# Features of the next batch in two-bank and single-bank PSUM tiles, and a product with Wa moved ahead of the ends

## The chip, the cores and the metric

The kernel runs on one core of a Trainium2 chip. The metric is the device time of one execution in microseconds; three runs of the kernel before gave 2164.74, 2165.57 and 2166.67, a median of 2165.57. The core has five queues that run in order: TensorE (PE) for matrix products and transposes, VectorE (DVE), ScalarE (ACT), GpSimd (POOL), which here only issues indirect DMAs, and SyncE (SP), which issues most plain DMAs.

## The reference

Two graph layers run over 16 batches of 1024 nodes with 256 features; `adj` is one sparse 1024x1024 matrix for all batches.

```python
feats = einsum('bni,oi->bno', data, W1)
f1 = einsum('bno,o->bn', feats, W2) + b2[0]
coefs = softmax(leaky_relu(f1[:, :, None] + f1[:, None, :]) + adj, axis=-1)
h = einsum('bij,bjo->bio', coefs, feats) + bias2 + data
# second layer, on h
pre_u = h @ W1[:d];  pre_v = h @ W1[d:]
S = sigmoid(relu(pre_u[:, :, None, :] + pre_v[:, None, :, :] + b1) @ W2 + b2)
a = einsum('buv,bud->bvd', S * adj, h)
m = einsum('uv,bud->bvd', adj, h) * h
z = beta1 * h + beta2 * (a @ Wa + ba) + beta3 * (m @ Wm + bm)
```

## The kernel before

**Order of the work.** The tile scheduler is switched off. A `Timetable` (line 347) keeps entries of a planned time and a function; `matmuls` (line 360) puts an entry at `now` and moves `now` on by the planned length of the columns. `run` sorts all entries by time and emits them. So the planned times fix only the order of the instructions on each queue; on the chip each queue runs in that order, as soon as its semaphores allow.

**Stages.** For every batch TensorE computes the features (`features`, line 986), eight chunks of 128 nodes in four pairs `c2`; each chunk is two matmuls (512 records in the trace for 256 matmuls) of 257 columns, 256 features and a last column that carries the node's logit. `keep_features` (line 999) clamps the last columns of a pair (`f`, VectorE, line 1004), takes an exponential of them (ScalarE, line 1008) and copies the two chunks to SBUF scaled by it (ScalarE, line 1016). `begin_f` (line 1389) turns the eight clamped columns into rows (`pr`, TensorE, line 965), takes their highest value (VectorE, line 973) and makes `row` and `col` (ScalarE, lines 979 to 984). `spread` (line 1023) makes eight weight tiles `eT` on VectorE; `attend` (line 1037, `pv`) multiplies them with the features; `keep_h` (line 1049) finishes a chunk of the layer's output h on VectorE.

Of h, `turn_h` (line 1057, `ph`) makes transposed pairs of chunks, copied by ScalarE (line 1072). For each pair i, `end` (line 1074, `pp`) computes the two products with the second layer's W1, side 0 copied by VectorE (line 1091) and side 1 by ScalarE (line 1093); `weighed` (line 1103, `pea`) computes the product with Wa, copied by ScalarE (line 1118). All three results go to DRAM through SP's queue. `message` (`pm`, line 1135) and `product` (`pz`, line 1154) make m and its product with Wm. Eight batches (`LATER`: 0 to 3 and 11 to 14) put the messages off to the end of the kernel, by storing h (`put_off`, line 1126); the others, 4 to 10, do them at once, spread over the next batch.

**Scores.** The edges of the graph are stored as 135 slots of 128 edges. For each of three groups of batches (0 to 4, 5 to 9, 10 to 15) and each slot, POOL gathers rows of the ends (`gv`, line 1200, and `gu`, line 1193), VectorE compares (line 1229), ScalarE reduces per batch (line 1243), and POOL scatters the results (line 1209). These steps are planned at an even pace over most of the kernel, so they stand between the other instructions of VectorE and ScalarE. The scores of a group start after its last batch; after the last batch, `gather` (line 1335, `pzg` and `pzh`) sums over scored edges.

**PSUM.** There are eight banks, in two pools: `p1` is a ring of four single banks (`pv`, `ph`, `pea`, `pm`, `pz`), `p2` a ring of two tiles of two banks each (transposed input `pt`, features `pf`, ends `pp`, rows `pr`, and `pzg` at the end). A new tile of a ring waits until the oldest one's readers are done.

**The place of the change** is the handover from batch b-1 to b. At the end of the pass for one batch, TensorE's order is: attention 6, `ph` (2), attention 7, the four pairs of features of the next batch, ends (2, 0), `ph` (3), `pr`. The next pass of the loop (line 1466) begins with `pea` (2), ends (2, 1), for batches 4 to 10 a message, ends (3, 0), ends (3, 1), `pea` (3), and then attention 0 of the new batch:

```python
weigh_ends(b - 1, 2)
one_end(b - 1, 2, 1)
if at_once:
    messages(b - 1, 0, 0)
one_end(b - 1, 3, 0)
one_end(b - 1, 3, 1)
weigh_ends(b - 1, 3)
```

In p2's ring the order here is: pairs 0 to 3, ends (2, 0), `pr`, ends (2, 1), (3, 0), (3, 1).

Of the kernel before, what the change touches and what calls it, by code (L numbers as in the profile page):

```python
# [8 lines left out]
F32 = mybir.dt.float32  # L9
AF = mybir.ActivationFunctionType  # L10
ALU = mybir.AluOpType
# [3 lines left out]
P = 128  # L15
BANK = 512
# [6 lines left out]
SPAN = 2500.0  # L23
# [348 lines left out]
def edge_layers(  # L372
# [36 lines left out]
    nc = tc.nc  # L409
    B, N, D = x.shape  # L410
# [10 lines left out]
    p1 = ctx.enter_context(tc.tile_pool(name="p1", bufs=4, space=PSUM))  # L421
    p2 = ctx.enter_context(tc.tile_pool(name="p2", bufs=2, space=PSUM))
# [484 lines left out]
    st = {}  # L907
# [76 lines left out]
        nc.scalar.activation(st["col"], st["f99"], AF.Exp, bias=st.pop("under"))  # L984

    def features(b, c2):
        pf = st["pf", c2] = p2.tile([P, 2, BANK], F32, tag="p2", name="pf")
        for i in range(2):
            c = 2 * c2 + i
            for h in range(H):  # L990
                nc.tensor.matmul(  # L991
                    pf[:, i, : D + 1],
                    lhsT=st["xT"][:, h, c * P : (c + 1) * P],
                    rhs=w1T[:, h, :],
                    start=(h == 0),
                    stop=(h == H - 1),
                )

    def keep_features(b, c2):
        if c2 == 0:  # L1000
            st["feats", b] = work.tile([P, C, D + 1], F32, name="feats")
            st["f99"] = two.tile([P, C], F32, name="f99")
        feats, f99, pf = st["feats", b], st["f99"], st.pop(("pf", c2))
        nc.vector.tensor_scalar(
            f99[:, 2 * c2 : 2 * c2 + 2], pf[:, :, D], -2.0 * SPAN, 2.0 * SPAN, ALU.max, ALU.min
        )

        nc.scalar.activation(
            feats[:, 2 * c2 : 2 * c2 + 2, D],
            f99[:, 2 * c2 : 2 * c2 + 2],  # L1010
            AF.Exp,
            scale=SLOPE / (1.0 - SLOPE),
        )
        for i in range(2):
            c = 2 * c2 + i
            nc.scalar.activation(  # L1016
                feats[:, c, :D], pf[:, i, :D], AF.Copy, scale=feats[:, c, D : D + 1]
            )
        if c2 == C // 2 - 1:
            nc.vector.tensor_tensor(f_most, f_most, f99, ALU.max)  # L1020
            nc.vector.tensor_tensor(f_least, f_least, f99, ALU.min)
# [52 lines left out]
    def end(b, i, side):  # L1074

        pp = st["pp", side] = p2.tile([P, 2, BANK], F32, tag="p2", name=f"pp{side}")
        for k in range(2):
            for h in range(H):
                nc.tensor.matmul(  # L1079
                    pp[:, k, :R],  # L1080
                    lhsT=st["hTi", b, i][:, h, k * P : (k + 1) * P],
                    rhs=wuv[:, side, h, :],
                    start=(h == 0),
                    stop=(h == H - 1),
                )

    def keep_end(b, i, side):
        e = two.tile([P, 2, R], F32, name=f"end{side}", tag="end", bufs=3)
        pp = st.pop(("pp", side))[:, :, :R]
        if side == 0:  # L1090
            nc.vector.tensor_tensor(e, pp, bu.unsqueeze(1).to_broadcast([P, 2, R]), ALU.add)
        else:
            nc.scalar.copy(e, pp)  # L1093
        g, j = member(b)
        rows = slice(2 * i * P, (2 * i + 2) * P)
        nc.sync.dma_start(
            out=(pu_d, pw_d)[side][g][rows, j * R : (j + 1) * R].rearrange(
                "(c p) k -> p c k", p=P
            ),
            in_=e,  # L1100
        )

    def weighed(b, i):
        pp = st["pea"] = p1.tile([P, 2, D], F32, tag="p1", name="pea")
        for k in range(2):
            for h in range(H):
                nc.tensor.matmul(  # L1107
                    pp[:, k, :],
                    lhsT=st["hTi", b, i][:, h, k * P : (k + 1) * P],
                    rhs=wa[:, h, :],  # L1110
                    start=(h == 0),
                    stop=(h == H - 1),
                )

    def keep_weighed(b, i):
        g, j = member(b)
        e = two.tile([P, 2, D], F32, name="ea")
        nc.scalar.copy(e, st.pop("pea"))
        nc.sync.dma_start(
            out=ha_d[g][2 * i * P : (2 * i + 2) * P, j * D : (j + 1) * D].rearrange(  # L1120
                "(c p) k -> p c k", p=P
            ),
            in_=e,
        )

    def put_off(b):

        nc.sync.dma_start(out=h_d[b], in_=held[b].rearrange("p c d -> p (c d)"))
# [6 lines left out]
    def message(b, half, h):  # L1135
        span = slice(half * BANK, (half + 1) * BANK)
        pm = st["pm", h] = p1.tile([P, BANK], F32, tag="p1", name="pm")
        for c in range(C):
            nc.tensor.matmul(  # L1139
                pm,  # L1140
                lhsT=held[b][:, c, h * P : (h + 1) * P],
                rhs=adj_sb[:, c, span],
                start=(c == 0),
                stop=(c == C - 1),
            )

    def keep_message(b, half, h):
        if h == 0:
            st["mT"] = dense.tile([P, H, BANK], F32, name="mT")
        nc.vector.tensor_tensor(  # L1150
            st["mT"][:, h, :], st.pop(("pm", h)), st["hT", b, half][:, h, :], ALU.mult
        )
# [252 lines left out]
    def grows(*chunks):  # L1405
        for c in chunks:
            end = times.matmuls(C * P, lambda c=c: turn_grown(c))
            times.at(end + 0.2, lambda c=c: keep_grown(c))

    def attention(b, c):  # L1410
        end = times.matmuls(C * (D + 1), lambda: attend(b, c))
        times.at(end + 0.6, lambda: keep_h(b, c))
# [5 lines left out]
    def one_end(b, i, side):  # L1418
        time = times.matmuls(4 * R, lambda: end(b, i, side))
        times.at(time + 0.3, lambda: keep_end(b, i, side))  # L1420

    def weigh_ends(b, i):
        time = times.matmuls(4 * D, lambda: weighed(b, i))
        times.at(time + 0.3, lambda: keep_weighed(b, i))
# [6 lines left out]
    def messages(b, half, h, delay=0.3):  # L1431
        time = times.matmuls(C * BANK, lambda: message(b, half, h))
        times.at(time + delay, lambda: keep_message(b, half, h))
# [32 lines left out]
    for b in range(B):  # L1466
        at_once = b > 0 and b - 1 not in LATER
        more = b + 1 < B

        if b:  # L1470
            weigh_ends(b - 1, 2)
            one_end(b - 1, 2, 1)
            if at_once:
                messages(b - 1, 0, 0)
            one_end(b - 1, 3, 0)
            one_end(b - 1, 3, 1)
            weigh_ends(b - 1, 3)
            if b - 1 in LATER:
                times.at(times.now, lambda b=b: put_off(b - 1))
            if any(b == lo for lo, _ in GROUPS):  # L1480
                started.append(times.now + 19.0)
        attention(b, 0)
        if b == 0:
            grows(6, 7)
        if at_once:
            messages(b - 1, 0, 1)
        attention(b, 1)
        spreads(b, 0)
        if more:
            times.at(times.now, lambda b=b: load_x(b + 1))  # L1490
        if at_once:
            products(b - 1, 0, 1)
        if b == 0:
            for i in range(2):
                for h in range(H):
                    times.matmuls(2 * R, lambda i=i, h=h: sort_columns(i, h))
            times.matmuls(2 * R, sort_bias)
        attention(b, 2)
        if at_once:
            messages(b - 1, 1, 0)  # L1500
        turned_ends(b, 0)
        attention(b, 3)
        spreads(b, 1)
        if at_once:
            messages(b - 1, 1, 1)
        both_ends(b, 0)
        attention(b, 4)
        if at_once:
            products(b - 1, 2, 3)
        if not more:  # L1510
            times.at(times.now, lambda: take_up(LATER[0]))
            times.at(times.now + 20.0, lambda: take_up(LATER[1]))
        turned_ends(b, 1)
        if more:
            begin(b + 1, 0)
        attention(b, 5)
        both_ends(b, 1)
        if more:
            begin(b + 1, 1)
        attention(b, 6)  # L1520
        turned_ends(b, 2)
        attention(b, 7)
        for c2 in range(C // 2):
            if more:
                begin_features(b + 1, c2)
        one_end(b, 2, 0)
        turned_ends(b, 3)
        if more:
            begin_f(b + 1)
# [58 lines left out]
    b = B - 1  # L1588
    for n in range(3):
# [5 lines left out]
        b = LATER[n]  # L1595
# [31 lines left out]
    for i, at in starts.items():  # L1627
        if i == 5:
            continue
        b = LATER[i]  # L1630
# [137 lines left out]
```

## Time and profile before

| | |
|---|---|
| median of three runs | 2165.57 us |
| the profiled execution | 2166.46 us, its span 2164.4 us |
| mean granted TensorE clock | 0.985 |
| DMA, whole span | 644.37 MB, 297 to 298 GB/s |
| DMA share 960 to 1080 us / 1500 to 1700 us | 0.82 / 1.00 |
| granted clock 1080 to 1150 us / 1290 to 1340 us | 0.93 / 1.00 |
| TensorE busy, 960 to 1080 us | 110.57 of 120 us |
| TensorE busy, 1290 to 1340 us | 50.00 of 50 us |

Times in the profile are counted from the start of the span. A line of a timeline has the start, the duration, the engine, the line of the kernel, the operation, what it writes and reads, and how many instructions were merged; a bracket gives the idle time before it and what ended it. A "remote" release is one whose queue the profile does not know. A line of waits names who waited for whom, with the total, the number and the longest. In a group's line, busy time and mean duration of one stand before the bar, and after it the engine's idle time just before those instructions, with its main releasers.

### The profile page before, as it was taken

The page shows a single profiled execution, that of the slowest core. Times are in us where ns is not written, and L with a number is a line of the kernel's source. Part 1 is how long each engine was busy: PE and PEld are TensorE (multiplying, and loading weights), DVE is VectorE, ACT ScalarE, POOL GpSimd, SP SyncE. Part 2 cuts the span into 40 slices and gives each one's busy share as a digit, 9 for nine tenths or more (in the row PEclk, how much of TensorE's full clock was granted, in tenths as well). Part 3 has the DMA queues.
Part 4 walks back from the last instruction along what each step waited for, and adds up shares of the span by engine and source line. Part 5 has one row for each costly group of instructions (what it writes and reads, how often), then busy time and mean ns, then how long its engine had stood idle before and what let it go on. Part 6 is the DMA issues. An engine that isn't in the chain of part 4 may idle for free.

```text
span 2164.4 us, 28928 instructions
## 1 busy us (share of the span) xinstructions
PE 2054.0 (95%) x8566; PEld 1561.6 (72%) x8566; DVE 1565.5 (72%) x2316; ACT 1378.6 (64%) x4842; POOL 1128.4 (52%) x986
## 2 busy tenths in 40 slices
PE   6999999999999999989899899999999999999998
PEld 5887888777676767667678777456666767667887
DVE  6798875577767676667667776577888978885544
ACT  4212222476767767576777787468888788885554
POOL 2121221267666676667666668665767666674000
PEclk8999999999999999999999999999999999999999
DMA  6587776788877787788888889899999999997774
GB/s 211 201 328 292 287 294 249 257 267 274 282 260 256 262 277 249 270 282 268 267 298 283 270 276 341 310 344 413 392 388 384 402 410 385 368 396 276 266 240 134
DMA packets 248007, 644.37 MB, mean 298 GB/s; under 512 B 37154, under 2 KB 137506, under 8 KB 245794
## 3 DMA queue, kind: packets, MB, share of 16 engines
q0 software_dynamic: 82528, 349.79, 46.4%
q1 hardware_dynamic: 129474, 258.44, 32.5%
q10 hardware_dynamic: 35840, 34.22, 4.6%
q8 instruction: 69, 1.13, 0.2%
q14 instruction: 96, 0.79, 0.1%
HBM read 479.56 MB, written 162.92 MB: 297 GB/s over the span
## 4 chain that ended last, share of the span: by engine, by line
PE 56%; DVE 15%; issue 9%; DMA 7%; ACT 7%; POOL 3%; another core or an unknown queue 2%; ACTq 0%; POOLq 0%; DVEq 0%
PE pv L1041 16%; PE pm L1139 10%; PE pp L1079 9%; PE pzg L1344 7%; DVE gv L1229 6%; DMA gv<-pw_d,idx_v 6%; ACT gv L1243 4%; PE pea L1107 4%; PE pf L991 3%; PE pzh L1344 3%; PE pz L1159 2%; DVE apart L1331 2%; POOL sa_d L1209 2%; POOL gv L1200 1%
## 5 line engine op out<-in xcount | busy, mean ns | idle before, releaser
L1243 ACT ACTIVATE gv<-gv 128x272 f32<-128x272 f32 x2058 | 856.4, 419 | 301.5 <-DVE gv L1229 152.6
L1229 DVE TENSOR_TENSOR gv<-gv,gu 128x680 f32<-128x680 f32 (+1 forms) x810 | 705.5, 907 | 106.3 <-DMA gv<-pw_d,idx_v 101.4
L1200 POOL DMA_INDIRECT gv<-pw_d,idx_v x405 | 481.1, 1188 | 386.3 <-ACT gv L1243 248.6
L1209 POOL DMA_INDIRECT sa_d<-lg,idx_s x405 | 496.1, 1225 | 131.5 <-issue 112.5
L1041 PE MATMUL pv<-feats,eT 128*128 128x257 f32 x2048 | 468.6, 381 | 5.1 <-DVE eT L1028 3.5
L1139 PE MATMUL pm<-adj_sb,xh 128*128 128x512 f32 x1024 | 450.0, 592 | 1.8 <-DVE xh L1055 1.8
L1041 PEld LDWEIGHTS pv<-feats,eT 128*128 128x128 f32 x2048 | 382.0, 190 | 67.6 <-DVE eT L1028 9.6
L1344 PE MATMUL pzg<-ha_g,apart 128*128 128x256 f32 x1536 | 370.5, 384 | 25.0 <-DVE apart L1331 18.3
L1243 ACT ACTIVATION_READ_ACCUMULATOR gv<-gv 128x1 f32 x2058 | 389.2, 189 | 0.0
L1344 PEld LDWEIGHTS pzg<-ha_g,apart 128*128 128x128 f32 x1536 | 287.7, 190 | 91.2 <-DVE apart L1331 35.6
L1139 PEld LDWEIGHTS pm<-adj_sb,xh 128*128 128x128 f32 x1024 | 193.1, 190 | 220.0 <-issue 217.2
L1326 ACT COPY apart<-sat 128x640 f32<-128x640 f32 (+1 forms) x192 | 264.4, 1391 | 87.8 <-PE pzh L1344 46.7
L1079 PE MATMUL pp<-wuv,hT 128*128 128x272 f32 x1024 | 257.9, 402 | 20.6 <-ACT end L1093 7.1
L1331 DVE TENSOR_TENSOR apart<-apart,adj_sb 128x640 f32<-128x640 f32 (+1 forms) x192 | 165.9, 866 | 118.0 <-ACT apart L1326 112.5
L1079 PEld LDWEIGHTS pp<-wuv,hT 128*128 128x128 f32 x1024 | 196.4, 194 | 75.6 <-ACT end L1093 10.4
L1028 DVE SCALAR_TENSOR_TENSOR eT<-row,col,grown 128x512 f32<-128x512 f32 x256 | 183.1, 745 | 28.0 <-ACT col L984 25.1
L843 POOL DMA_INDIRECT table_d<-rec,at x52 | 57.5, 1106 | 267.2 <-DVE rec L836 160.4
L991 PE MATMUL pf<-w1T,xT 128*128 128x257 f32 x512 | 128.6, 405 | 30.6 <-ACT feats L1016 25.5
L1072 ACT COPY hT<-ph 128x512 f32<-128x512 f32 x96 | 55.2, 576 | 147.8 <-PE ph L1061 90.3
L991 PEld LDWEIGHTS pf<-w1T,xT 128*128 128x128 f32 x512 | 101.5, 202 | 54.5 <-ACT feats L1016 32.9
L1159 PE MATMUL pz<-wm,mT 128*128 128x256 f32 x512 | 118.1, 384 | 6.0 <-DVE mT L1150 5.3
L1107 PE MATMUL pea<-wa,hT 128*128 128x256 f32 x512 | 122.3, 382 | 0.0
(184 smaller groups left out, 1616.2 us busy)
## 6 DMA issues: line engine op xcount, KB each, us to landing
sa_d<-zero SPq DMA_DIRECT2D x128, 512.0 KB
sat<-sa_d SPq DMA_DIRECT2D x128, 320.0 KB
sat<-sa_d SPq DMA_DIRECT2D x64, 384.0 KB
pu_d<-end SPq DMA_DIRECT2D x64, 272.0 KB
pw_d<-end SPq DMA_DIRECT2D x64, 272.0 KB
xh<-in_x_dram SPq DMA_DIRECT2D x16, 1024.0 KB
ha_d<-ea SPq DMA_DIRECT2D x64, 256.0 KB
zb_d<-zb ACTq DMA_DIRECT2D x64, 256.0 KB
```

The costliest lines, as they stand in the source:

```text
L991: nc.tensor.matmul(pf[:, i, : D + 1], lhsT=st["xT"][:, h, c * P : (c + 1) * P], rhs=w1T[:, h, :], start=(h == 0), stop=(h == H - 1),)
L1041: nc.tensor.matmul(pv[:, : D + 1], lhsT=st["eT", b, k, j // 4][:, j % 4, i * P : (i + 1) * P], rhs=st["feats", b][:, j, :], start=(j == 0) ...
L1079: nc.tensor.matmul(pp[:, k, :R], lhsT=st["hTi", b, i][:, h, k * P : (k + 1) * P], rhs=wuv[:, side, h, :], start=(h == 0), stop=(h == H - 1),)
L1107: nc.tensor.matmul(pp[:, k, :], lhsT=st["hTi", b, i][:, h, k * P : (k + 1) * P], rhs=wa[:, h, :], start=(h == 0), stop=(h == H - 1),)
L1139: nc.tensor.matmul(pm, lhsT=held[b][:, c, h * P : (h + 1) * P], rhs=adj_sb[:, c, span], start=(c == 0), stop=(c == C - 1),)
L1200: nc.gpsimd.indirect_dma_start(out=gv, out_offset=None, in_=pw_d[g], in_offset=bass.IndirectOffsetOnAxis(ap=idx_v[:, t, s : s + 1], axis=0),)
L1209: dma = nc.gpsimd.indirect_dma_start(out=sa_d[g], out_offset=bass.IndirectOffsetOnAxis(ap=idx_s[:, t, s : s + 1], axis=0), in_=lg[:, i, : ...
L1229: nc.vector.tensor_tensor(mv, mv, mu, op)
L1243: nc.scalar.activation(one[:, j, :], one[:, j, :], AF.Copy, accum_out=lg[:, i, j : j + 1])
L1326: nc.scalar.copy(apart.rearrange("p g v -> p v g"), sat)
L1331: nc.vector.tensor_tensor(apart, apart, a.unsqueeze(1).to_broadcast([P, SIZE[g], P]), ALU.mult)
L1344: nc.tensor.matmul(st["pzg", g, vc][j // 4][:, j % 4, :], lhsT=apart[:, j, :], rhs=ha, start=(c == 0 and j % 2 == 0), stop=(c == C - 1 and ...
```

## The change

In `features`, pairs 0 and 1 stay in two-bank tiles of p2. Each chunk of pairs 2 and 3 gets a single bank of p1, four in all. `keep_features` clamps the last column of both chunks of a pair in one VectorE instruction where they share a tile, and in two instructions of one column each where they don't. The rest of it is the same, with another operand. In the handover, `pea` (3) is emitted ahead of ends (3, 0) and (3, 1) where the batch's messages are put off, and stays behind them where they are made at once.

```diff
     def features(b, c2):
-        pf = st["pf", c2] = p2.tile([P, 2, BANK], F32, tag="p2", name="pf")
+        if c2 < 2:
+            both = p2.tile([P, 2, BANK], F32, tag="p2", name="pf")
+            pfs = [both[:, 0, : D + 1], both[:, 1, : D + 1]]
+            st["pf", c2] = [both[:, :, D]], pfs
+        else:
+            pfs = [p1.tile([P, BANK], F32, tag="p1", name="pf1")[:, : D + 1] for _ in range(2)]
+            st["pf", c2] = [pf[:, D:] for pf in pfs], pfs
...
-                    pf[:, i, : D + 1],
+                    pfs[i],
...
-        feats, f99, pf = st["feats", b], st["f99"], st.pop(("pf", c2))
-        nc.vector.tensor_scalar(
-            f99[:, 2 * c2 : 2 * c2 + 2], pf[:, :, D], -2.0 * SPAN, 2.0 * SPAN, ALU.max, ALU.min
-        )
+        feats, f99 = st["feats", b], st["f99"]
+        lasts, pfs = st.pop(("pf", c2))
+        n = 2 // len(lasts)
+        for i, column in enumerate(lasts):
+            at = 2 * c2 + n * i
+            nc.vector.tensor_scalar(
+                f99[:, at : at + n], column, -2.0 * SPAN, 2.0 * SPAN, ALU.max, ALU.min
+            )
...
-                feats[:, c, :D], pf[:, i, :D], AF.Copy, scale=feats[:, c, D : D + 1]
+                feats[:, c, :D], pfs[i][:, :D], AF.Copy, scale=feats[:, c, D : D + 1]
...
             if at_once:
                 messages(b - 1, 0, 0)
+            else:
+                weigh_ends(b - 1, 3)
             one_end(b - 1, 3, 0)
             one_end(b - 1, 3, 1)
-            weigh_ends(b - 1, 3)
+            if at_once:
+                weigh_ends(b - 1, 3)
```

## The prediction

> **What bounds the kernel now.** I read the page first, then TensorE's waits, then TensorE's timeline at all 15 places where one batch hands over to the next, then VectorE's and ScalarE's timelines there.
>
> ```profile
> span 2164.4 us, 28928 instructions
> PE 2054.0 (95%) x8566; PEld 1561.6 (72%) x8566; DVE 1565.5 (72%) x2316; ACT 1378.6 (64%) x4842; POOL 1128.4 (52%) x986
> L991 PE MATMUL pf<-w1T,xT 128*128 128x257 f32 x512 | 128.6, 405 | 30.6 <-ACT feats L1016 25.5
> ```
>
> TensorE is busy 95% of the span. What it loses is in short waits, and the features (pf, L991) hold the largest single share. From TensorE's waits (total, times, longest):
>
> ```profile
> PE pf L991 <- ACT feats L1016: 25.5, 13, 6.4
> PE pp L1079 <- ACT end L1093: 7.1, 7, 2.2
> PE pp L1079 <- ACT row L979: 6.9, 4, 2.9
> PE pf L991 <- DVE gv L1229: 3.6, 1, 3.6
> ```
>
> These four make 43.1 us, and each is a wait for one of the two buffers of the two-bank pool p2. TensorE's timeline at the handover to batch 12 (start, duration, idle before in brackets):
>
> ```profile
> 1047.74 3.64 PE L991 MATMUL pf<-w1T,xT 128*128 128x257 f32 x16
> 1057.73 5.79 PE L991 MATMUL pf<-w1T,xT 128*128 128x257 f32 x16 [6.36 <-ACT feats L1016]
> 1065.20 0.60 PE L1061 MATMUL ph<-ident,xh 128*128 128x128 f32 x4
> 1074.17 2.10 PE L1079 MATMUL pp<-wuv,hT 128*128 128x272 f32 x8 [1.81 <-ACT end L1093]
> 1077.83 10.60 PE L1041 MATMUL pv<-feats,eT 128*128 128x257 f32 x48
> ```
>
> Pairs 0 and 1 of the features run at once; pair 2 waits until ScalarE has copied pair 0 out. After the wait the same 16 matmuls take 5.79 us and not 3.64, at a lower granted clock. On VectorE and ScalarE:
>
> ```profile
> 1053.90 0.48 DVE L1055 SCALAR_TENSOR_TENSOR xh<-pv,inv,xh 128x256 f32<-128x256 f32 x1
> 1056.41 0.16 DVE L1004 TENSOR_SCALAR f<-pf 128x2 f32<-128x2 f32 x1 [2.02 <-remote]
> 1061.56 0.16 DVE L1004 TENSOR_SCALAR f<-pf 128x2 f32<-128x2 f32 x1 [2.78 <-PE pf L991]
> ```
> ```profile
> 1056.84 0.84 ACT L1016 ACTIVATE feats<-pf,feats 128x256 f32<-128x256 f32 x2
> 1061.75 0.20 ACT L1008 ACTIVATE feats<-f 128x2 f32<-128x2 f32 x1 [0.64 <-DVE f L1004]
> ```
>
> The clamp f of pair 0 stands behind score work and comes 5 us late; then VectorE waits 2.78 us for pair 2, which TensorE could not begin. Each engine waits in turn for the other.
>
> **What a handover costs now.** Without waits, the steps from the first feature matmul take (gaps of starts in the handover to batch 1, 93.95 to 113.32): four pairs 6.96, ends (2,0) 1.83, ph 0.44, pr 0.87, pea 1.73, ends (2,1) 1.83, which is 13.66; then ends (3,0) and (3,1) 3.67 and pea 1.73, 19.06 to the next attention. Measured less these: batch 1 0.3; 2 to 4: 4.3, 2.3, 2.3; 5 to 7: 0.2, 0.4, 1.0; 8 to 11: 5.2, 4.0, 5.5, 1.7; 12 to 15: 11.0, 12.2, 10.9, 7.7. The sum is 69 us, the ceiling of any gain here.
>
> **The change part by part.**
>
> *Single banks.* Pairs 2 and 3 no longer wait for p2. In p1's ring of four, their chunks take the banks of pea (1), pv (6), ph (2) and pv (7). The youngest is pv (7), released by VectorE at 1054.38 in the handover to batch 12, where chunk 7 would start at 1053.83: 0.55 us late. Before, pair 2 waited for copies that stand behind that same release, so this wait is looser in every handover.
>
> What is late next: ends (2,0) need pair 0's bank pair; ph needs chunk 4's bank, pea (2) chunk 5's; pr needs all clamps. Batch 8, worked out: pair 0 starts at 638.53, four pairs end at 645.49, pair 0 was copied at 645.36, so ends (2,0) run 645.49 to 647.32. ScalarE's copy of pair 1 ends at 647.55, two or three reductions of scores follow to 648.36, then exp and the first copy to 649.05; ph starts at 649.05 where it started at 652.50: 3.4 us gained of 5.2. The same steps give batch 9 2.6 (ph 749.65 for 752.22), batch 10 3.8 (850.2 for 854.0), batch 11 1.7 (VectorE's 1.59 us wait for pair 2 goes), together 11.5. Batches 1, 5, 6, 7: all of their excess at most, 0.1 + 0.2 + 0.4 + 1.0 = 1.7.
>
> *Clamps.* Pairs 2 and 3 take two 128x1 clamps each, not one of 128x2: two more per batch. A 128x1 from PSUM stands in the trace as the reciprocal inv, 164 ns; f itself takes 156. So 0.16 us each, 2 x 15 x 0.16 = 4.8 us on VectorE. Between nothing (VectorE is waiting anyway, 43.8 us for pf in all) and 4.8 I take 2.4.
>
> *The product in front of ends (3,0)*, in the eight handovers with a put-off batch (1 to 4, 12 to 15). It issues 8 matmul records (1.73 us), a ScalarE copy (574 ns) and a store on SP, which now go ahead of the two ends with their copies and stores. On SP the ends' two stores queue behind the product's wait for ScalarE; no gather of the group reads them soon, since no group ends with a put-off batch but the last, whose last batch isn't moved. The 1.73 us cover the waits for row (2.11, 0.93, 0.93, 2.91) and for end (three times 0.16, then 1.81, 1.99, 2.21, 0.58): up to 5.3 + 6.2 = 11.5 us. The next attention loses that cover: it now follows end (3,1), and it needs eight eT tiles from VectorE. In batches 2 to 4 and 15 it was held by those already (first three attentions 11.46 us for 10.44). There only what eT gains counts: VectorE's end (0.72 us) goes behind two eT tiles, and the chain of pr, under, row, col moves by what the features gain: 1.8 (1.26 us of feature wait and part of 0.72), 1.2, 1.2, and 1.3 for batch 15. Batches 12 to 14 get both: ph 1061.8 for 1065.2, with eT some 3 us earlier: 3.2; batch 13, where the last two waits in the features (1.70, 3.03) and three slow stretches fall together: 5.0 (ph 1132.2 for 1137.6); batch 14 4.5. Together 4.2 + 14.0 = 18.2.
>
> Sum: 11.5 + 1.7 + 18.2 - 2.4 = 29.0 us. What comes earlier meets the gathers earlier: VectorE waited 101.4 us for them in 46 waits, 2.2 us each. I count half of one such wait in half of eight handovers, 4.4 us (bounds 0, and 8 x 2.2 = 17.6): 24.6 us remain, 11.4 to 29.
>
> The waits also set the clock: four feature stretches after waits of 3.24 to 6.36 us took 5.38 to 5.79 us for 3.64 (+7.5 in all); with later slow stretches I count 15.9 us, and where a wait shrinks below some 2 us its share is in the differences above. The Trainium skill (TensorE: Matmul & The Clock Gate, "What's actually happening") says that the array falls to half rate after an idle window of about 3.4 us; by it only the three waits above that would be slow, some 5.7 us. The trace has a slow stretch after 1.99 us too (1146.44, 3.22 us for 2.00), so the row decides.
>
> From the profiled execution (2166.46, of which the span is 2164.4): 2166.46 - 24.6 = 2141.9. The median, 2165.57, is 0.9 lower: **2141 us**. Nothing between 1340 us and the end is changed; the orders of all queues stay, so a lead there is carried on, if the scores have it too.
>
> **Rivals.**
> *All waits go* (0.08): the four rows, 43.1 us, and the slow stretches, 15.9, are gone and the chains behind keep pace: 2107. Against it: ScalarE's copies stand in order behind score work and bind ph.
> *The wait only moves* (0.15): ph and pr wait for the copies as long as pair 2 did. Then only the moved product counts, half of 11.5, less 2.4: about 2162. For it: ScalarE's 49.9 us of waiting for f. Against: VectorE and ScalarE themselves wait for pf (2.78, 0.64 above).
> *The scores keep the end* (0.09): SP stands 16.93 us at 1961.23 for the last scatters, and TensorE waits 1.60 and 1.20 us there, so nothing is spare. If the scores of the last group end at 1976 as now (the DMA share is 1.00 from 1500 to 1900), the lead is lost: 2165. Against: score steps stand in the same queues as the features, and POOL waits 248.6 us for ScalarE.
> *Slower* (0.08): the 30 clamps stand on the path, ahead of exp, copy and ph, from the point where ph waits for ScalarE in every handover and the lead doesn't reach the end: +4.8, 2170.
> *It doesn't do what it says*: if p1's banks came free later than p2's, pair 2 would still wait; the releases above exclude it.
>
> **Chances.** Forecast 0.60 (own range 2126 to 2155). Faster by over 0.2% (4.3 us, about what a measurement can tell from no change): 0.60 + 0.08 + 0.09 of the moved wait = 0.77; within: 0.06 of the moved wait + 0.06 of the scores = 0.12; slower: 0.08 + 0.03 = 0.11. The range 2122 to 2166 takes in the forecast, the moved wait and most of the third rival.
>
> **What would show it.** Right: pf L991 waits under 5 us in all, mean of a pf matmul near 385 ns; new waits of ph or pea for ACT feats L1016, 1 to 3 us each, in batches 8 to 14; pp waits for row and end nearly gone; attention waits for eT grow a little; the last phase as long as before. Wrong: the pf waits stand at ph in full length, gather waits of VectorE well over 101 us, or a longer wait at about 1950.

## The result, and the profile after

The changed kernel took 2141.44 us, median of 22 runs (2129.88 to 2156.17). The kernel before, run beside it, took 2156.7 us, median of 22 runs (2146.61 to 2166.67). The ratio is 0.9928 with a 95% interval of 0.9909 to 0.9947: faster by 15.3 us between the medians, or by 11 to 20 us by the interval. The forecast of 2141 us, faster, holds.

Two things stand beside that at once. First, the three runs shown ahead of the change (2164.74 to 2166.67) lay at the top of what that kernel does: the later median is 9 us below them. The forecast took 24.6 us from a baseline that was about 9 us too high, and the true gain is about 9 us smaller. So it is luck that the time came out to half a microsecond: two errors of about 9 us cancel. Second, the profiled execution after took 2134.4 us, 7 us *below* its median, where the one before lay 9.8 us above its own. So the two profiles differ by 31.7 us of span, twice what the kernels differ by. They are read here for the mechanism, and the sizes are taken from the runs.

The page after (span, busy times, the group of the features):

```profile
span 2132.7 us, 28964 instructions
PE 2041.3 (96%) x8566; PEld 1555.2 (73%) x8566; DVE 1566.5 (73%) x2348; ACT 1373.8 (64%) x4842; POOL 1119.9 (53%) x986
L997 PE MATMUL pf<-w1T,xT 128*128 128x257 f32 x512 | 118.2, 386 | 3.2 <-issue 1.6
```

The features' idle time went from 30.6 to 3.2 us, and the mean of a feature matmul from 405 to 386 ns. TensorE's busy time is 12.7 us smaller for the same 8566 records, because fewer stretches run at a low clock: the granted clock from 960 to 1340 us is 0.99, where it was 0.96. TensorE's waits after (total, times, longest):

```profile
PE pv L1051 <- DVE eT L1038: 9.0, 9, 3.5
...
PE pp L1089 <- ACT end L1103: 6.8, 5, 2.2
...
PE pp L1089 <- ACT feats L1026: 4.8, 4, 2.2
PE ph L1071 <- ACT feats L1026: 4.4, 3, 1.5
...
PE pp L1089 <- ACT row L979: 0.4, 1, 0.4
```

The 25.5 us for which pf waited for feats are gone. In their place ends (2, 0) and `ph` wait for the same copies, 9.2 us together: the copies are still late, but about a third of the wait is left. The wait for `row` fell from 6.9 to 0.4 us, the wait for `end` stayed (7.1, now 6.8), and the attention's wait for `eT` rose from 3.5 to 9.0. TensorE's timeline at the handover to batch 12:

```profile
1032.53 3.64 PE L997 MATMUL pf<-w1T,xT 128*128 128x257 f32 x16
...
1038.47 5.10 PE L997 MATMUL pf<-w1T,xT 128*128 128x257 f32 x14 [0.35 <-issue]
1045.03 2.10 PE L1089 MATMUL pp<-wuv,hT 128*128 128x272 f32 x8 [1.45 <-ACT feats L1026]
1048.63 0.66 PE L1071 MATMUL ph<-ident,xh 128*128 128x128 f32 x4 [1.51 <-ACT feats L1026]
...
1059.04 2.10 PE L1089 MATMUL pp<-wuv,hT 128*128 128x272 f32 x8 [1.75 <-ACT end L1103]
1060.98 3.21 PE L1051 MATMUL pv<-feats,eT 128*128 128x257 f32 x14
1064.80 7.66 PE L1051 MATMUL pv<-feats,eT 128*128 128x257 f32 x34 [0.62 <-DVE eT L1038]
```

The wait of 6.36 us before pair 2 is gone; 1.45 and 1.51 us stand where the copies are needed next. The moved product ran before the last two ends, but the wait for `end` is still there (1.75), and the attention now waits 0.62 for `eT`, which it did not before. From the first feature matmul to the attention this handover took 28.45 us, where it took 30.09.

Measured in the way of the prediction (from the start of the features to the start of the next attention, or of the message in batches 5 to 11, less the dense 19.06 or 13.66 us), all handovers of these two profiles and of some of the runs that follow compare as below. *Between* is the sum over 14 batches from the start of attention 0 to the start of the next features, so it holds what lies outside the handovers. All columns are worked out from TensorE's timelines and are good to 0.1 us.

| excess, us | 1 | 2 to 4 | 5 to 7 | 8 to 11 | 12 to 15 | sum | between |
|---|---|---|---|---|---|---|---|
| before | 0.3 | 8.9 | 1.6 | 16.5 | 41.8 | 69.1 | 794.8 |
| after | 0.2 | 1.1 | 0 | 2.5 | 25.0 | 28.7 | 808.0 |
| single banks alone (`banks`) | 0.3 | 7.3 | 0 | 6.3 | 27.1 | 40.9 | 797.6 |
| moved product alone (`move`) | 0.2 | 3.9 | 1.6 | 18.7 | 28.5 | 53.0 | 805.3 |
| changed kernel again (`full`) | 0.2 | 1.0 | 0 | 6.3 | 26.7 | 34.3 | 818.2 |
| before, on another chip (`before_again`) | 0.3 | 8.9 | 1.0 | 3.3 | 15.7 | 29.2 | 784.9 |
| the same without the scores (`bare_before`) | 0.3 | 10.1 | 0.2 | 0 | 0 | 10.6 | 778.3 |

From before to after, the handovers gave 40.4 us and the stretches between them took back 13.2. In the second profile of the changed kernel, the longest of its 12 runs (2159.83 us), they gave 34.9 and took back 23.4. Not every column can be read alike. Batches 2 to 4 repeat from profile to profile (8.9 in both of before, 1.1 and 1.0 in both of after). Batches 12 to 15 don't: with the moved product alone, which took no less time than before, they show 28.5 us where before has 41.8. A difference of some 13 us in that column is not by itself a gain of the change. In the profile after nothing is lost behind 1333 us: the stage from the first `pe` matmul to the end, in which nothing is changed, took 799.4 us (1333.30 to 2132.7), before 807.5. In `full` it took 811.6, so it too varies by 12 us between profiles.

### The profile page after: what moved, and what is told of

Same layout as the page of the kernel before. It is cut to its first block, busy times and chain, and to the rows that moved or that the text cites. A ratio compares the mean times of both kernels' runs of the same rounds, so it can differ in the third digit from the quotient of the medians.

```text
span 2132.7 us, 28964 instructions
## 1 busy us (share of the span) xinstructions
PE 2041.3 (96%) x8566; PEld 1555.2 (73%) x8566; DVE 1566.5 (73%) x2348; ACT 1373.8 (64%) x4842; POOL 1119.9 (53%) x986
## 4 chain that ended last, share of the span: by engine, by line
PE 66%; DVE 13%; ACT 7%; DMA 7%; issue 5%; POOL 1%; another core or an unknown queue 0%; POOLq 0%; ACTq 0%; SPq 0%; DVEq 0%
PE pv L1051 18%; PE pm L1149 13%; PE pp L1089 8%; PE pzg L1354 8%; DVE gv L1239 5%; PE pf L997 4%; PE pea L1117 4%; ACT gv L1253 4%; PE pz L1169 3%; PE pzh L1354 3%; DMA gv<-pw_d,idx_v 3%; DVE eT L1038 2%; DVE apart L1341 2%; ACT apart L1336 2%; DMA xh<-in_x_dram 1%
## 5 line engine op out<-in xcount | busy, mean ns | idle before, releaser
L1239 DVE TENSOR_TENSOR gv<-gv,gu 128x680 f32<-128x680 f32 (+1 forms) x810 | 705.6, 907 | 105.1 <-DMA gv<-pw_d,idx_v 89.3
L1089 PE MATMUL pp<-wuv,hT 128*128 128x272 f32 x1024 | 252.6, 396 | 16.6 <-ACT end L1103 6.8
L1082 ACT COPY hT<-ph 128x512 f32<-128x512 f32 x96 | 55.1, 575 | 134.0 <-PE ph L1071 103.5
L997 PE MATMUL pf<-w1T,xT 128*128 128x257 f32 x512 | 118.2, 386 | 3.2 <-issue 1.6
L1354 PE MATMUL pzh<-ha_g,apart 128*128 128x256 f32 x384 | 114.7, 380 | 0.0
```

What stands on the lines that cost most here:

```text
L1089: nc.tensor.matmul(pp[:, k, :R], lhsT=st["hTi", b, i][:, h, k * P : (k + 1) * P], rhs=wuv[:, side, h, :], start=(h == 0), stop=(h == H - 1),)
L1239: nc.vector.tensor_tensor(mv, mv, mu, op)
L1354: nc.tensor.matmul(st["pzg", g, vc][j // 4][:, j % 4, :], lhsT=apart[:, j, :], rhs=ha, start=(c == 0 and j % 2 == 0), stop=(c == C - 1 and ...
```

## Experiments

The runs were on three chips. On the chip of the first four the kernel before takes 2158.1 us (median of 35 runs); on the chip of the next four 2114.07 (7 runs, 2109.8 to 2115.77); on that of the last four 2113.52 (21 runs, 2108.2 to 2116.65). A ratio always compares runs of one chip.

**The two parts, each alone.** `full` is the changed kernel without an edit. `banks` has the features' edit, and the product stays behind the ends:

```diff
             if at_once:
                 messages(b - 1, 0, 0)
-            else:
-                weigh_ends(b - 1, 3)
             one_end(b - 1, 3, 0)
             one_end(b - 1, 3, 1)
-            if at_once:
-                weigh_ends(b - 1, 3)
+            weigh_ends(b - 1, 3)
```

`move` has that hunk of the change and the features of before. `early` is the changed kernel with the clamps and copies planned ahead of the score work they stood behind:

```diff
-        times.at(end + 0.3, lambda: keep_features(b, c2))
+        times.at(end - 0.9, lambda: keep_features(b, c2))
```

> The changed kernel once more, beside its parts on one chip. Both theories: ratio to the kernel before 0.989 to 0.996, the waits of pf for ScalarE's copies gone.

> Only the single banks for pairs 2 and 3; pea (3) stays behind the ends. Theory A (both parts count, the banks for two thirds): 0.992 to 0.996 of the kernel before, pf waits under 5 us in all, pp waits for row and end stay near 14 us. Theory B (the whole gain comes from the banks, the moved product gives nothing since the attention then waits for eT): the same ratio as the full change, within 0.2%. Theory C (the gain comes from the moved product): 0.998 to 1.002, with the wait of pf found again at ph and pp.

> Only the product in front of the ends; the features as before. Theory A: 0.996 to 0.999, pf waits as before (20 to 30 us), pp waits for row and end under 7 us. Theory B: 0.999 to 1.002, with pv waiting for eT by as much as pp gained. Theory C: as the full change.

> The changed kernel with the features' clamp, exponential and copies planned 1.2 us earlier, so that they stand ahead of some score work in VectorE's and ScalarE's queues. If what is left of the wait (ph and pp for the copies, 9 us in the profile after) comes from score work that stands ahead: 0.995 to 0.999 of the changed kernel, those waits under 5 us. If the score work is held up behind clamps that wait for the matmuls: 1.000 to 1.006 of it, VectorE's wait of f for pf grows from 21 us to over 35.

| run | median us | ratio to before | 95% interval |
|---|---|---|---|
| full | 2143.28 | 0.9936 | 0.9910 to 0.9961 |
| banks | 2142.62 | 0.9937 | 0.9905 to 0.9968 |
| move | 2160.58 | 1.0014 | 0.9985 to 1.0042 |
| early | 2142.07 | 0.9929 | 0.9902 to 0.9956 |

The single banks alone give what the whole change gives (0.9937 and 0.9936). The moved product alone shows no gain: +2.4 us between the medians, and the interval reaches from 3 us faster to 9 us slower. TensorE's waits in `banks`, then in `move`:

```profile
PE pp L1089 <- ACT end L1103: 6.8, 5, 2.5
PE pp L1089 <- ACT row L979: 6.8, 5, 2.1
...
PE pv L1051 <- DVE eT L1038: 3.8, 2, 3.5
```
```profile
PE pf L991 <- ACT feats L1016: 16.4, 9, 5.0
PE pv L1041 <- DVE eT L1028: 7.7, 7, 3.5
```

The group of the features in the same two runs:

```profile
L997 PE MATMUL pf<-w1T,xT 128*128 128x257 f32 x512 | 115.2, 380 | 2.8 <-issue 1.9
```
```profile
L991 PE MATMUL pf<-w1T,xT 128*128 128x257 f32 x512 | 127.4, 402 | 26.6 <-ACT feats L1016 16.4
```

With the single banks alone, the waits of `pp` for `row` and `end` stand as before, the wait for `eT` is short, and pf's idle time is as low as in the whole change: 2.8 us, with a mean of 380 ns for a feature matmul.

With the moved product alone, `row` is gone from the list (6.9 us before) and `eT` has grown from 3.5 to 7.7: the wait is now one step later. In batches 2 to 4, where the table repeats, what was won comes back in full: the excess fell by 5.0 us (8.9 to 3.9), and the three stretches from attention 0 to the next features grew by 5.0 together (from 42.5 or 42.6 us each to 44.2 or 44.3). `early` can't be told from `full`. It took the waits of `pp` for feats off the list and left `ph` 3.8 us of 4.4, yet its time, which was expected to be 0.995 to 0.999 of that of `full`, is the same within the interval.

**The same without the scores.** The scores' reductions and compares stand between the copies on ScalarE and VectorE. With the loop over the slots empty in `scores`, the time is that of the rest alone:

```diff
-        for k in range(len(SLOTS)):
+        for k in ():
```

`bare_before`, `bare_banks` and `bare_move` have this edit in the kernel before, in `banks` and in `move`. `before_again` is the kernel before without an edit, once, with a profile from this chip.

> The kernel before with the score steps of all three groups left out (no gathers of the ends, no compares, reductions or scatters; the rest of the kernel sums over zeros). Theory A (score work that stands ahead of the clamps and copies in VectorE's and ScalarE's queues makes pair 2 wait): the waits of pf for ScalarE's copies fall from 25.5 us to under 4 in all. Rival (two tiles of p2 are too few whatever else runs): they stay above 12 us.

> The same without scores, with the single banks alone. Theory A: 1 to 6 us under bare_before. Rival: 12 us or more under it.

> The same without scores, with the moved product alone. If the attention needs eT no later than the product would have kept TensorE busy (the product only changes places with the wait): within 2 us of bare_before, pp waits for row and end fall and waits of pv for eT rise by the same. If it covers the waits for good: 5 to 12 us under bare_before.

> The kernel before once more, for a second profile. If the profile that the prediction was made from is a typical execution: about 2158 us with the handovers' excess over their dense length near 69 us in sum. If it was an execution with long gathers: a shorter time, and an excess of 50 to 60 us.

| run | median us (range) |
|---|---|
| bare_before | 2042.18 (2041.57 to 2042.58) |
| bare_banks | 2038.17 (2037.89 to 2038.6) |
| bare_move | 2042.49 (2041.88 to 2043.18) |
| before_again | 2111.39 (one run) |

Runs of one of these kernels differ by about 1 us, so fractions of a per cent can be read. Without the scores the single banks are worth 4.0 us, and the moved product costs 0.3. TensorE's waits of `bare_before`, then of `bare_move`:

```profile
PE pp L1079 <- ACT row L979: 4.0, 3, 2.1
PE pv L1041 <- DVE eT L1028: 3.1, 1, 3.1
PE pf L991 <- ACT feats L1016: 2.1, 3, 1.3
```
```profile
PE pv L1041 <- DVE eT L1028: 6.1, 7, 3.0
...
PE pp L1079 <- ACT row L979: 0.4, 1, 0.4
```

The wait of pf for feats is 2.1 us here. In the whole kernel it is 8.2 on this chip (`before_again`, below) and 25.5 in the profile before. The excess of batches 5 to 15 is 0.2 us here and 20.0 in the whole kernel on this chip. So nearly all lateness in these batches comes with the scores, as the prediction read from the clamp that came 5 us late. Without the scores their gathers and scatters are gone too, so these runs don't tell the score instructions in the queues from the transfers that they wait for. Of the 15.5 us that `banks` gained on the other chip 4.0 are left; `banks` with the scores was not run on this chip, so a part of that difference may be the chip's.

The moved product takes 3.6 us from the wait for `row` and gives 3.0 to the wait for `eT`. The wait for `end` is only 0.3 us in `bare_before`, so what this pair tests is the wait for `row`. The handover to batch 3 shows how. TensorE's timelines of `bare_before` and `bare_move`:

```profile
236.83 2.10 PE L1079 MATMUL pp<-wuv,hT 128*128 128x272 f32 x8 [0.93 <-ACT row L979]
...
241.03 1.89 PE L1107 MATMUL pea<-wa,hT 128*128 128x256 f32 x8
242.75 3.69 PE L1041 MATMUL pv<-feats,eT 128*128 128x257 f32 x13
```
```profile
235.49 1.89 PE L1107 MATMUL pea<-wa,hT 128*128 128x256 f32 x8
...
240.89 1.03 PE L1041 MATMUL pv<-feats,eT 128*128 128x257 f32 x4
242.43 2.69 PE L1041 MATMUL pv<-feats,eT 128*128 128x257 f32 x8 [0.51 <-DVE eT L1028]
```

The product fills the wait of 0.93 us, and the attention starts 1.86 us earlier, against tiles `eT` that VectorE has not made yet; it then waits in pieces of half a microsecond. Over all handovers the moved product takes 6.3 us off the excess (10.6 to 4.3) and puts 6.0 on the stretches between (778.3 to 784.3).

`before_again` shows how far the waits depend on the run and the chip. The same kernel, with the same order of all queues:

```profile
PE pp L1079 <- ACT end L1093: 8.2, 7, 2.2
PE pf L991 <- ACT feats L1016: 8.2, 10, 1.8
```

Here pf waits 8.2 us for feats, not 25.5, and the excess of all handovers is 29.2 us, not 69.1 and not the 50 to 60 that were expected of a shorter execution. Nearly all of the difference lies in batches 8 to 15.

**On a chip with short waits, and the eT tiles closer.** If the excess is only 29.2 us on a faster chip, the change should be worth less there. `full_again` is the changed kernel on such a chip. In `early_et` the eight tiles of the first attention are planned 0.3 us apart, so that fewer compares stand between them; `banks_et` is that without the moved product, `both_et` that with the edit of `early`:

```diff
-            times.at(end + (3.0 if b else 4.2) + (0.8 if b else 0.5) * j, lambda j=j: spread(b, 0, j))
+            times.at(end + (3.0 if b else 4.2) + (0.3 if b else 0.5) * j, lambda j=j: spread(b, 0, j))
```

> The changed kernel a third time, beside the next three. If the gain is what late copies cost in the handovers, it follows the kernel before on the same chip: where that takes about 2158 us, 12 to 18 us; where it takes about 2114 us, 4 to 12 us. If the gain is structural and the same everywhere: about 15 us on any chip.

> The changed kernel with the eight eT tiles of a handover planned 0.3 us apart and not 0.8, ahead of score compares (or of the building of the edge list) on VectorE. If the moved product gave nothing because the attention then waits for eT: 3 to 10 us under the changed kernel, waits of pv for eT under 4 us (9.0 in the profile after), the stretch from one attention 0 to the next features back near 42 us in batches 2 to 4. If VectorE has no room and the held-up compares delay the gathers: equal or slower.

> Single banks and closer eT tiles, without the moved product. If the moved product pays once eT is early: 3 to 8 us slower than the run with the moved product and closer eT. If closer eT alone is what helps: the same as that run.

> The changed kernel with closer eT tiles and the features' clamps and copies planned 1.2 us earlier. If both waits come from score work standing ahead: the fastest of these four, 5 to 14 us under the changed kernel. If not: within 3 us of the run with closer eT alone.

| run | median us | ratio to before | 95% interval |
|---|---|---|---|
| full_again | 2100.15 | 0.9939 | 0.9925 to 0.9954 |
| early_et | 2102.87 | 0.9954 | 0.9938 to 0.9971 |
| banks_et | 2107.38 | 0.9979 | 0.9967 to 0.9991 |
| both_et | 2107.56 | 0.9972 | 0.9959 to 0.9986 |

The change is worth 13.4 us here (10 to 16 by the interval), beside 14.8 on the slower chip (8 to 19). Expected were 4 to 12 us if the gain follows the waits, and about 15 if it doesn't. The excess of the handovers fell from 29.2 (`before_again`) to 8.2 us, by 21.0, and the stretches between took back 12.6 (784.9 to 797.5), so 8.4 us of the lead stand at the last handover by these two profiles, which are of two chips. So the gain does not shrink as the excess in the two profiles of before does (69.1 and 29.2). Whether it shrinks a little the intervals can't tell, and why it doesn't shrink more is open.

Closer `eT` tiles do a part of what they were put there for, and do not pay. TensorE's wait for `eT` is 10.2 us in `full_again` and 6.7 in `early_et`, where under 4 was expected; the stretches after attention 0 in batches 2 to 4 fell from 44.3 to 43.6 us, not to 42. VectorE's waits for gathered rows in its list of waits (total, times, longest), in the same order:

```profile
DVE gv L1239 <- DMA gv<-pw_d,idx_v: 110.8, 46, 12.1
```
```profile
DVE gv L1239 <- DMA gv<-pw_d,idx_v: 138.1, 60, 12.0
```

TensorE gains 3.5 us at `eT`; VectorE's waits for gathers grow by 27.3. The same row is 135.5 in `both_et` and 117.6 in `banks_et`. One profile each is no proof of the cause. None of the three beats the changed kernel, the fastest of the kernels timed on that chip; `banks_et` and `both_et` are slower than it, with intervals that do not overlap, and `early_et` can't be told from it. `both_et` was expected to be the fastest and is not.

With early `eT` the moved product is worth 4.5 us between the medians (2107.38 less 2102.87), inside the 3 to 8 that were expected if it pays then. Both ratios share the runs of before, so the two kernels are better compared run with run: the means of 12 and 6 runs are 4.8 us apart, with a standard error of 1.6. So here the moved product seems to pay, while the closer tiles themselves bring nothing (`early_et` is 2.7 us above `full_again`). Against it stands `both_et`, which has the moved product too and is as slow as `banks_et`, unless its earlier clamps cost as much again. How the single banks and the moved product share the 13.4 us on this chip is not known, since neither was run alone on it.

## Why the prediction held, and which step did not

**What bounded the kernel** was read rightly. Pair 2 waited for a copy that stood behind score work, and both engines then waited in turn. Two details differ: pair 0 was computed at 1049.64, so its clamp at 1056.41 came 6.8 us late and not 5, and in the last 2.02 of these VectorE was idle, released by a "remote", which is not score work ahead in its queue. With four more banks for the features pf's wait went, and with it most of the low clock behind it. The Trainium skill (Perfetto Trace Analysis, "Matmul Optimizations") advises to use all eight PSUM banks, so that more instructions can be under way. The runs here agree for the features, which went from four banks to eight (the kernel as a whole had all eight in use before): `banks` gains 15.5 us of 2158.1. They also bound it: without the scores' work ahead of the copies, on another chip, the same banks are worth 4.0 us of 2042.18.

**The single banks (11.5 + 1.7 us).** In the profiles, handovers 8 to 11 lost 14.0 us of their excess (10.2 by the banks alone, none by the moved product alone) and batches 1 and 5 to 7 lost 1.7. (The sum counted 0.1 us for batch 1, where its own list has 0.3.) What is late next was named rightly: ends (2, 0) and `ph` waited for feats, 4.8 and 4.4 us, no wait over 2.2. `pea`, which was named too, did not wait.

**The product in front of ends (3, 0): this is the step that failed.** The prediction said that the 1.73 us cover the waits for `row` and `end`, "up to 5.3 + 6.2 = 11.5 us", that "batches 12 to 14 get both", and put 18.2 us to it together with the features' gain in these batches. In the form in which it was predicted, the runs show no gain from the moved product: 1.0014 alone (0.9985 to 1.0042), +0.3 us without scores, no difference between `full` and `banks`. These intervals leave room for a few microseconds in the whole kernel, not for 11. Two of its parts fell:

- Batches 2 to 4 were costed by "only what eT gains counts", 4.2 us. The handovers there lost 7.9 us of excess, 1.6 of it by the banks alone. Of the other 6.2, 5.0 came back: from attention 0 to the next features each of the three batches took 1.6 to 1.7 us more (42.5 to 42.6 before, 44.2 to 44.3 after), which is nearly the cover of 1.73 us that the attention lost. Some 1 us is left of the 4.2.
- In batches 12 to 15 the handovers lost 16.8 us of excess. With the banks alone they lost 14.7, and with the moved product alone, at no gain in time, 13.3, so this column moves too much between executions to size either part. The wait for `end` did not go (7.1 to 6.8 in all). The prediction counted here what the features' gain brings together with what the product covers, and the runs find the time with the banks alone.

So the working was right to set what is covered against what is uncovered, and wrong to book to the product more than the difference, which is near 0 as long as `eT` comes no earlier. With closer `eT` tiles, on another chip, it seems to be 4.5 us.

**The clamps (2.4 us)** were sized rightly as instructions: a 128x1 clamp takes 153 ns in the mean of 64 in the profile after, for the 160 assumed. Whether they cost anything on the path can't be told: no run had the clamps without the banks.

**The gathers (4.4 us)** meet an earlier lead, the prediction said. In the profile after VectorE waits less for them, not more: 89.3 us in 41 waits, where it was 101.4 in 46. But the same kernel before has 117.3 in the other chip's profile, and `move`, which gained nothing, 80.9, so this row moves more from run to run than by the change, and the term is neither shown nor refuted.

**The size.** The sum, 29.0 us, was a reading of one execution whose waits were long. For that execution it is near: in the two profiles the stage's end at 1333 us moved by 23.5 us, for 24.6 forecast. The other 8.2 us between the spans lie behind it, where nothing was changed. That the total is near although the product's part failed is again luck: the handovers gave more than was counted (40.4 us), and the stretches between them took back more (13.2, for 4.4 counted). Against the medians of 22 runs the forecast gain is too large by 9 us, and the baseline was too high by as much.

**The rivals.** "The wait only moves" (2162) is refuted: 9.2 us of waits for feats remain of 25.5, and `banks` alone gains. It was right about the other half of the change, where the wait did little but move. "The scores keep the end" (2165) is refuted: the lead at 1333 us is carried to the end. "All waits go" (2107) is refuted by the 28.7 us of excess that remain, 25.0 of them in batches 12 to 15. "Slower" (2170) and "It doesn't do what it says" are refuted by the time and by pf's row.

**The signs that were named.** pf's waits under 5 us (3.2) and a mean near 385 ns (386) came. New waits of 1 to 3 us came at `ph` and ends (2, 0). `eT` grew (3.5 to 9.0), by more than the little that was named. "pp waits for row and end nearly gone" came for `row` and not for `end`. The last phase is not longer.

## What to carry to other kernels

When a matrix product waits for its PSUM buffer, look at what stands ahead of the releasing copy in its engine's queue: here the extra banks were worth 4 us without the score work ahead of the copies and 15 us with it (on two chips, so the chip is in that difference too). Moving an instruction into a wait gains only if the place that it leaves had no wait of its own to hide: put the cover won and the cover lost into one line, and follow it to the next wait before writing a gain. Before a sum is made from one profiled execution, set its time against the spread of the runs, and remember that a few runs close together (2164.74 to 2166.67) may all lie at one end of it.

## What the runs showed of the hardware that was not expected

- The same kernel takes 2158.1 us on one chip and 2114.07 and 2113.52 on two others, 2% apart, with runs that do not overlap (from 2148.92 up, and up to 2116.65). The granted clock over the span is 0.985 and 0.994 in the two profiles of before, and TensorE's busy time 2054.0 and 2033.3 us for the same 8566 records, so a longer busy time of TensorE makes 20.7 of the 55.1 us between these two spans. What in the chips makes the difference is open.
- The spread within one chip goes with the scores: 35 runs of the kernel before lie between 2148.92 and 2177.04, those of one kernel without scores within 1.3 us. On one chip (before 2114, without scores 2042) the scores cost 72 us in all; the spread was some 6 us there over 7 runs.
- The clock fell after short waits too, and the length of one wait does not decide it. In the profile before a wait of 3.28 us at 746.31 was followed by 16 feature matmuls in 3.79 us, at a granted clock of 1.00, and one of 3.24 us at 645.40 by 16 in 5.42. In the handover to batch 12 of the profile after, waits of 0.15, 0.96 and 0.35 us within 2.3 us stand ahead of the feature matmuls from 1038.47 on, which took 5.10 us for 14, where 16 took 3.64; the windows (time, TensorE busy, clock, DMA share, GB/s) show the half-idle stretch and the fall behind it:

```profile
1036.00:1039.00 3.00, 1.54 (x6) 1.00 0.76 246
1039.00:1045.00 6.00, 4.57 (x13) 0.72 0.75 233
```

- In the same place VectorE starts the clamp of pair 0 at 1043.70, where the trace names TensorE's features as the release (2.21 us of waiting), though pair 0 was computed at 1034.43 and pair 1 at 1036.17. TensorE's 0.96 us at 1037.75 and a wait of 1.18 us of ScalarE at 1039.31 are put down to "issue", so in this stretch three engines stand still for nothing that the profile shows. The execution before has a wait of 2.02 us at the same clamp, released by a "remote". What holds this clamp is not shown by either trace; it makes a part of the 25.0 us that batches 12 to 15 still lose.
